# A second written order for the steps of a conv and state-space kernel

## The chip, the cores and the metric

The kernel runs on one core of a Trainium2 chip. The metric is the device time in microseconds of one execution; three runs are given as their median and their range. A profile of one further execution shows every instruction with its start and its length. Five engines work side by side, each with an in-order queue of its own: TensorE (PE in the profile) multiplies matrices, VectorE (DVE) and ScalarE (ACT) work element by element and read TensorE's results, GpSimd (POOL) works element by element on on-chip memory, and SyncE (SP) issues the DMA transfers.

## The reference

The input is x of shape 128 x 128 x 16 x 16 (batch, channels, height, width), in float32. Two layers follow each other.

Layer 0 is a group norm followed by a quantised residual block: batch norm, clipping and rounding to 4 bits, a 3x3 convolution with 4-bit weights masked by a cross pattern, the same again with a diagonal pattern, and two residual additions.

Layer 1 takes each image as 256 tokens of 128 channels:

```python
t = _to_tokens(x)
t = t + mamba(_ln_t(t), fwd weights) + reversed(mamba(reversed(_ln_t(t)), bwd weights))
t = t + moe(_ln_t(t))
x = _from_tokens(t, x)
```

One direction of `mamba` projects the tokens to z, x, B, C and a step size dt; runs a causal convolution of four taps and a silu over x, B and C; takes a softplus of dt; then computes a scan with decay in chunks (as matrix products with an exponential mask), adds D times x, multiplies by silu(z), normalises by the root mean square and projects back to 128 channels with four heads of 64. `moe` is a router over eight experts that keeps the best two of them for each token and mixes their 128 x 128 linear maps with softmax weights.

## The kernel before, in words

Layer 0 runs first, about 300 us, with the whole batch held on chip as 64 tiles of two images; it isn't touched by the change, and neither is any instruction of layer 1.

Layer 1 works on 64 pairs of images (512 tokens each). The work on one pair is written as generators, the `part_...` functions. Each `yield` ends a *step*: a group of instructions that all go to one engine's queue. The parts that matter here:

- `part_a`: load of the pair's tokens, layer norm, transposition to `uT`. `part_c` handles two pairs at once: dt, softplus, logarithms and cumulated sums (`dt` and `r_ps` matmuls), then DMAs that build the rows and columns of the decay mask.
- `part_x` (L821), for direction d and channel block n: one matmul step of 128x512 in float32 into a PSUM bank, one ScalarE step and three VectorE steps (`x1`, `x2`, `x3` below) that are the four taps. The bank is free after the third. `part_z` (L864): a matmul into such a bank, and a silu on ScalarE.
- `part_s` (L905): the mask's exponent as bf16 matmuls into such a bank, then an exponential on ScalarE. `part_g` (L890): the products of B and C, on 64 of the array's 128 rows. `part_m`: VectorE multiplies the two. `part_xt`: four transposes.
- `part_y` (L939): the scan's products, on 64 of the array's 128 columns (128x64), sixteen matmul records; then VectorE adds D times x, GpSimd multiplies by z, ScalarE squares. `part_n`, `part_r`: the root mean square (matmuls on 32 columns, `n` below; then a transpose). `part_o`: the projection back.
- `part_e` (L1024), a long chain: layer norm, transposition (`u2T`), router matmul on 32 columns (`rt`), transpose, then some twenty short VectorE steps on 128x32 values that find the best two experts (`lg`, `mx0`, `sel0`, `seld0`, `fi0`, `sele0`, `lgm`, `mx1`, `sel1`, ..., `g1`, `gt`), one GpSimd power, a transpose (`gtT`), and a DMA of the gates to DRAM. `part_p` loads the gates of two experts spread over all partitions (`gb`) and multiplies them by `u2T` on GpSimd, in two steps. `part_f` (L1116): the residual's transpose (`fT`) and eight expert matmul steps (`f0` to `f7`) into one bank, then out.

PSUM banks come from three rotating sets (L653): two banks for `x`, `z` and `s`, two for `y` and `f`, four for the rest. A matmul step that wants a bank waits until the bank's last reader is done.

The order is written out by hand in the table `T`. For each part it has two lists of places, one for even and one for odd pairs; the place of a step of pair i is `i // 2 * PERIOD` plus the number in the table, with `PERIOD = 372`. A period holds exactly 372 steps, those of two pairs at different stages, so a place is a rank and not a time:

```python
steps += [(i // 2 * PERIOD + t, len(steps) + n, stream) for n, t in enumerate(places[i % 2])]
steps.sort(key=lambda step: step[:2])
```

The steps are then issued in this order (`manual_schedule`), and each engine's queue has its own steps in the order of the places. Waits between engines are put in for data and for buffers.

Of the kernel before, what the change touches and what calls it, by code (L numbers as in the profile page):

```python
# [34 lines left out]
def kernel(ctx: ExitStack, tc: tile.TileContext, a: dict):  # L35
# [311 lines left out]
    with tc.tile_pool(name="w1p", bufs=1) as w1p:  # L347
# [15 lines left out]
        with tc.tile_pool(name="setup1", bufs=1) as setup, tc.tile_pool(  # L363
# [50 lines left out]
            for c in range(4):  # L414
# [34 lines left out]
                n = cuts[c + 1] - cuts[c]  # L449
# [666 lines left out]
    def part_f(i):  # L1116
# [7 lines left out]
        for e in range(NE):  # L1124
# [9 lines left out]

    PERIOD = 372
    T = {
        ('a',): [[72, 128, 230, 236, 267, 307], [250, 319, 407, 437, 469, 473]],
        ('c',): [
            [482, 492, 505, 516, 529, 550, 558, 571, 574, 577, 597, 603, 610, 617, 646, 648, 649, 656, 658,
             668, 688, 695, 706, 723, 727, 752, 774, 785, 887, 997],  # L1140
        ],
        ('x', 0, 0): [[662, 669, 670, 684, 685], [844, 852, 856, 859, 865]],
        ('x', 0, 2): [[693, 694, 700, 703, 712], [874, 881, 889, 890, 891]],
        ('x', 0, 1): [[714, 722, 733, 739, 740], [904, 908, 913, 915, 926]],
        ('x', 1, 2): [[750, 755, 764, 776, 788], [934, 945, 948, 952, 959]],
        ('x', 1, 0): [[771, 775, 790, 792, 797], [960, 968, 973, 978, 981]],
        ('x', 1, 1): [[811, 818, 823, 827, 830], [1001, 1007, 1019, 1023, 1027]],
        ('z', 1, 0): [[836, 839], [1031, 1035]],
        ('bc',): [[858, 892], [1046, 1055]],
        ('sx', 0): [[860], [1059]],  # L1150
        ('z', 0, 0): [[851, 853], [1038, 1043]],
        ('sx', 1): [[868], [1062]],
        ('z', 1, 1): [[863, 867], [1047, 1053]],
        ('z', 0, 1): [[878, 883], [1068, 1077]],
        ('g', 0): [[895], [1110]],
        ('s', 0, 0, 0): [[884, 885], [1079, 1080]],
        ('xt', 0, 0): [[910, 918], [1082, 1114]],
        ('s', 0, 1, 0): [[898, 903], [1083, 1089]],
        ('s', 0, 0, 1): [[909, 914], [1093, 1103]],
        ('s', 0, 0, 2): [[917, 923], [1104, 1121]],  # L1160
        ('m', 0, 0): [[931, 947], [1120, 1130]],
        ('xt', 1, 0): [[905, 935], [1132, 1153]],
        ('s', 0, 1, 1): [[933, 941], [1117, 1126]],
        ('s', 1, 1, 0): [[942, 953], [1133, 1141]],
        ('s', 0, 1, 2): [[967, 970], [1161, 1165]],
        ('xt', 0, 1): [[936, 958], [1088, 1125]],
        ('s', 1, 0, 2): [[1005, 1008], [1173, 1178]],
        ('g', 1): [[996], [1177]],
        ('m', 0, 1): [[1006, 1009], [1189, 1191]],
        ('s', 1, 0, 0): [[979, 988], [1166, 1171]],  # L1170
        ('s', 1, 1, 1): [[998, 999], [1193, 1196]],
        ('xt', 1, 1): [[1000, 1003], [1187, 1192]],
        ('s', 1, 0, 1): [[987, 991], [1182, 1184]],
        ('m', 1, 1): [[1037, 1045], [1209, 1218]],
        ('s', 1, 1, 2): [[1014, 1026], [1201, 1210]],
        ('y', 0, 1): [[1012, 1022, 1025, 1087], [1200, 1204, 1219, 1258]],
        ('y', 0, 0): [[1024, 1029, 1032, 1106], [1207, 1212, 1220, 1269]],
        ('m', 1, 0): [[1017, 1036], [1198, 1221]],
        ('y', 1, 1): [[1052, 1064, 1108, 1113], [1233, 1241, 1254, 1293]],
        ('y', 1, 0): [[1070, 1098, 1109, 1118], [1251, 1278, 1297, 1300]],  # L1180
        ('n', 0): [[1123], [1301]],
        ('n', 1): [[1131], [1312]],
        ('r',): [[1134, 1145, 1149, 1152, 1158], [1322, 1334, 1336, 1338, 1349]],
        ('o', 0): [[1155, 1172], [1337, 1356]],
        ('o', 1): [[1163, 1174], [1348, 1357]],
        ('e',): [
            [1185, 1203, 1205, 1215, 1222, 1227, 1229, 1243, 1245, 1247, 1248, 1266, 1268, 1271, 1272, 1274,
             1284, 1299, 1304, 1310, 1311, 1323, 1326, 1327, 1328, 1329, 1333, 1343, 1344, 1355, 1365],
            [1374, 1387, 1388, 1405, 1411, 1416, 1420, 1441, 1443, 1446, 1448, 1457, 1462, 1464, 1473, 1474,
             1479, 1488, 1491, 1500, 1501, 1507, 1509, 1510, 1512, 1516, 1522, 1526, 1528, 1531, 1540],  # L1190
        ],
        ('p', 0): [[1422, 1433, 1463], [1542, 1578, 1586]],
        ('p', 1): [[1367, 1421, 1426], [1624, 1651, 1655]],
        ('f',): [
            [1445, 1453, 1468, 1469, 1487, 1511, 1548, 1558, 1566, 1569, 1681],
            [1614, 1637, 1660, 1664, 1668, 1688, 1707, 1734, 1754, 1757, 1802],
        ],
        ('p', 2): [[1376, 1472, 1539], [1551, 1606, 1610]],
        ('p', 3): [[1514, 1547, 1552], [1663, 1730, 1736]],
    }  # L1200
    parts = {
        "a": part_a, "c": part_c, "x": part_x, "bc": part_bc, "sx": part_sx, "z": part_z, "xt": part_xt, "g": part_g,
# [45 lines left out]
```

## Time and profile before

| What | us |
|---|---|
| median of three runs | 2683.2 |
| range of the runs | 2682.34 to 2685.82 |
| the profiled execution | 2683.28 |
| its span in the profile | 2681.6 |
| TensorE matmuls busy | 2524.4 |
| VectorE busy | 2386.9 |
| ScalarE busy | 2043.1 |
| GpSimd busy | 1660.4 |

The span runs from the first to the last instruction; the rest of the execution's time lies around it. A busy time is the sum of the times at which an engine has a record; the records of neighbouring instructions can overlap, and the end of a matmul is modelled. In lines of the profile, `out<-in` names tiles, `128*64` behind a matmul is the part of the array that it uses (rows by columns), L is a line of the kernel, and a bracket holds the idle time ahead of an instruction and what ended it.

### The profile page before, as it was taken

Reading aid. Unit: us, or ns where it says so; the run is one execution under the profiler, and the core shown is the slowest. Engines: PE = TensorE matmul, PEld = TensorE weight load, DVE = VectorE, ACT = ScalarE, POOL = GpSimd, SP = SyncE. Lnnn points to the kernel's source line nnn. Section 1 sums busy time; section 2 is a strip of 40 time slices with the busy share of each in tenths; the row PEclk is TensorE's granted clock in tenths of the full one; section 3 lists DMA queues with packets and bytes.
Section 4 is the critical chain, followed back from the end, with each engine's and each line's share of the span. In section 5 each row is a group of like instructions: output and inputs, shape, how many; then the busy total and the mean of one; then the engine's idle time right before and its main releaser. Section 6 shows DMA issues by size and latency. Waiting matters only on the chain.

```text
span 2681.6 us, 47685 instructions
## 1 busy us (share of the span) xinstructions
PE 2524.4 (94%) x16004; PEld 1488.5 (56%) x16004; DVE 2386.9 (89%) x6161; ACT 2043.1 (76%) x3682; POOL 1660.4 (62%) x1728
## 2 busy tenths in 40 slices
PE   0889589999999999999999999999999999999997
PEld 0335245556566665666666556666665666666663
DVE  8877589999999999999999999999999999999884
ACT  6877478887777778777777887777778877777771
POOL 1876315666666666666666666666666666666666
PEclk9989799999999999999999999999999999999998
DMA  8458311332333222333332232323223233232223
GB/s 273 154 201 286 120 35 60 90 94 85 96 90 95 78 86 97 89 93 96 93 94 79 88 95 86 95 92 93 81 84 96 91 90 97 92 96 81 77 88 105
DMA packets 165706, 275.58 MB, mean 103 GB/s; under 512 B 46529, under 2 KB 89537, under 8 KB 165441
## 3 DMA queue, kind: packets, MB, share of 16 engines
q1 hardware_dynamic: 165440, 272.32, 32.6%
q8 instruction: 132, 2.16, 0.3%
q14 instruction: 134, 1.09, 0.1%
HBM read 197.45 MB, written 58.03 MB: 95 GB/s over the span
## 4 chain that ended last, share of the span: by engine, by line
PE 65%; DVE 26%; DMA 3%; issue 2%; ACT 2%; POOL 1%; SPq 0%; DVEq 0%; POOLq 0%; ACTq 0%
PE f_ps L1125 12%; PE x_ps L824 9%; PE o_ps L1008 8%; DVE xc L842 6%; PE y_ps L948 6%; PE z_ps L867 5%; PE cv L221 4%; PE sg L913 3%; DVE yg L960 3%; PE xt_ps L879 3%; PE g_ps L898 3%; PE y_ps L954 3%; DVE bc L842 3%; PE sg L915 2%; DMA xr<-in_x 2%
## 5 line engine op out<-in xcount | busy, mean ns | idle before, releaser
L842 DVE SCALAR_TENSOR_TENSOR xc<-x_ps,cw,xc 128x510 f32<-128x510 f32 (+2 forms) x768 | 570.3, 743 | 99.1 <-ACT xc L836 86.4
L1113 POOL TENSOR_TENSOR gb<-gb,u2T 128x512 f32<-128x512 f32 x512 | 639.8, 1276 | 13.7 <-DMA gb<-gd 12.8
L964 POOL TENSOR_TENSOR yg<-yg,z 128x512 f32<-128x512 f32 x256 | 328.0, 1281 | 502.8 <-DVE yg L960 502.8
L675 ACT ACTIVATE e<-sg 128x512 f32<-128x512 f32 x768 | 449.8, 594 | 223.6 <-PE sg L913 152.7
L1125 PE MATMUL f_ps<-gb,ew 128*128 128x512 f32 x1024 | 524.7, 607 | 3.5 <-POOL gb L1113 3.4
L824 PE MATMUL x_ps<-uT,wx 128*128 128x512 f32 x768 | 403.9, 608 | 9.7 <-DVE bc L842 4.4
L948 PE MATMUL y_ps<-e,xt 128*64 128x256 f32 x2048 | 321.0, 392 | 0.2 <-DVE yg L960 0.2
L929 DVE TENSOR_TENSOR e<-e,g_ps 128x1024 f32<-128x1024 f32 x256 | 310.0, 1211 | 2.8 <-PE g_ps L898 2.8
L842 DVE SCALAR_TENSOR_TENSOR bc<-x_ps,cw,bc 128x510 f32<-128x510 f32 (+2 forms) x384 | 285.1, 742 | 9.0 <-ACT bc L836 3.2
L836 ACT ACTIVATE xc<-x_ps,cb,cw 128x512 f32<-128x512 f32 x256 | 199.1, 778 | 118.1 <-PE x_ps L824 109.6
L867 PE MATMUL z_ps<-uT,wz 128*128 128x512 f32 x512 | 274.9, 619 | 1.3 <-DVE xc L842 1.2
L1008 PE MATMUL o_ps<-wo,yg 128*128 128x128 f32 x2048 | 249.9, 275 | 0.0
L1008 PEld LDWEIGHTS o_ps<-wo,yg 128*128 128x128 f32 x2048 | 239.3, 192 | 19.0 <-DVE sel L1093 17.3
L1125 PEld LDWEIGHTS f_ps<-gb,ew 128*128 128x128 f32 x1024 | 174.3, 192 | 90.5 <-issue 71.4
L973 POOL TENSOR_TENSOR sq<-sq,sq 128x512 f32<-128x512 f32 x128 | 163.3, 1276 | 72.3 <-ACT sq L967 72.2
L954 PE MATMUL y_ps<-e,xt 128*64 128x128 f32 x2048 | 198.9, 273 | 0.0
L960 DVE SCALAR_TENSOR_TENSOR yg<-xc,dcol,y_ps 128x512 f32<-128x512 f32 x256 | 189.1, 739 | 9.7 <-PE y_ps L954 9.7
L221 PE MATMUL cv<-hpad,wq 128*128 128x512 bf16 x640 | 179.4, 423 | 19.2 <-DVE hpad L194 9.7
L913 PE MATMUL sg<-rows,cols 128*128 128x256 bf16 x1024 | 191.5, 274 | 4.7 <-ACT e L675 3.1
L675 ACT ACTIVATE z<-z_ps 128x512 f32<-128x512 f32 x256 | 153.3, 599 | 52.1 <-PE z_ps L867 41.4
L954 PEld LDWEIGHTS y_ps<-e,xt 128*64 128x64 f32 x2048 | 147.0, 137 | 74.1 <-DVE e L934 0.4
L879 PEld LDWEIGHTS xt_ps<-ident,xc 128*128 128x128 f32 x1024 | 128.2, 141 | 105.4 <-issue 99.6
(255 smaller groups left out, 4869.0 us busy)
## 6 DMA issues: line engine op xcount, KB each, us to landing
gb<-gd SPq DMA_DIRECT2D x256, 512.0 KB
xr<-in_x SPq DMA_DIRECT2D x64, 256.0 KB
y<-yt SPq DMA_DIRECT2D x64, 256.0 KB
yt<-y SPq DMA_DIRECT2D x64, 256.0 KB
cc<-bc SPq DMA_DIRECT2D x128, 128.0 KB
out<-ob SPq DMA_DIRECT2D x64, 256.0 KB
o<-o SPq DMA_DIRECT2D x59, 256.0 KB
q<-o SPq DMA_DIRECT2D x59, 256.0 KB
```

The lines of the kernel that those rows point to most:

```text
L221: nc.tensor.matmul(ps, wq[:, tap, q, :], low(hp)[:, :, dy : dy + 16, dx : dx + 16], start=(n == 0), stop=(n == len(passes) - 1),)
L675: nc.scalar.activation(out, in_, func)
L824: nc.tensor.matmul(ps, wx[d][:, n * P : (n + 1) * P], uTs[i], start=True, stop=True)
L842: nc.vector.scalar_tensor_tensor(acc[:, :, to], raw[:, :, of], cw[:, d, n, 3 - back : 4 - back], acc[:, :, to], ALU.mult, ALU.add,)
L867: nc.tensor.matmul(ps, wz[:, d, n * P : (n + 1) * P], uTs[i], start=True, stop=True)
L929: nc.vector.tensor_tensor(e0.rearrange("p h t l -> p h (t l)"), e0.rearrange("p h t l -> p h (t l)"), gps[i, d, k][:, 0:NT].unsqueeze(1).t ...
L948: nc.tensor.matmul(y_ps[64 * q : 64 * q + 64, k, :], xt[:, 2 * k + s0, 64 * h : 64 * h + 64], e0[:, h].rearrange("p t l -> p (t l)"), star ...
L954: nc.tensor.matmul(y_ps[64 * q : 64 * q + 64, k, s1 * P : (s1 + 1) * P], xt[:, 2 * k + s1, 64 * h : 64 * h + 64], e1[:, h, :], start=False ...
L964: nc.gpsimd.tensor_tensor(yg, yg, zs[i, d][:, n, :], ALU.mult)
L1008: nc.tensor.matmul(o_ps[:, (2 * j + d) * P : (2 * j + d + 1) * P], ygs[i, d, n][:, t * P : (t + 1) * P], wo[d][:, n, :], start=(n == 0), s ...
L1113: nc.gpsimd.tensor_tensor(gb[:, e], gb[:, e], u2Ts[i], ALU.mult)
L1125: nc.tensor.matmul(f_ps, ew[:, e, :], gbs[i, e], start=False, stop=(e == NE - 1))
```

## The change

Every list in `T` is replaced: the same parts and the same number of steps in each, at other places. `PERIOD`, the parts and all other code stay. The rows that are spoken of later:

```diff
-        ('x', 0, 2): [[693, 694, 700, 703, 712], [874, 881, 889, 890, 891]],
-        ('x', 0, 1): [[714, 722, 733, 739, 740], [904, 908, 913, 915, 926]],
-        ('x', 1, 2): [[750, 755, 764, 776, 788], [934, 945, 948, 952, 959]],
...
+        ('x', 0, 2): [[799, 803, 811, 815, 817], [973, 983, 994, 996, 999]],
+        ('x', 0, 1): [[829, 835, 848, 849, 857], [1012, 1026, 1033, 1042, 1044]],
+        ('x', 1, 2): [[871, 876, 882, 888, 892], [1048, 1057, 1063, 1064, 1070]],
...
-        ('y', 0, 1): [[1012, 1022, 1025, 1087], [1200, 1204, 1219, 1258]],
-        ('y', 0, 0): [[1024, 1029, 1032, 1106], [1207, 1212, 1220, 1269]],
...
+        ('y', 0, 1): [[1126, 1149, 1156, 1167], [1311, 1320, 1327, 1407]],
+        ('y', 0, 0): [[1130, 1146, 1147, 1172], [1310, 1319, 1326, 1342]],
...
+        ('p', 0): [[1484, 1505, 1508], [1667, 1678, 1690]],
+        ('p', 1): [[1500, 1569, 1591], [1703, 1735, 1757]],
         ('f',): [
...
+            [1554, 1568, 1580, 1607, 1610, 1624, 1651, 1661, 1671, 1677, 1679],
+            [1721, 1752, 1764, 1768, 1783, 1810, 1835, 1855, 1866, 1868, 1895],
         ],
...
+        ('p', 2): [[1556, 1619, 1648], [1730, 1762, 1817]],
+        ('p', 3): [[1649, 1652, 1670], [1772, 1842, 1850]],
```

Sorted by place, TensorE's steps of one period in the repeating middle of the layer are these 103, first before and then after. Steps on a part of the array are in capitals with a star (`Y*` 128x64, `G*` 64x128, `N*`, `RT*`, `DT*` 128x32); `dtT`, `nT`, `rtT`, `gtT` are single transposes:

```
before:
s x xt s N* f4 x nT o gtT s o s s f5 G* s x f6 xt s f7 Y* s Y* z uT u2T x z DT* RT* Y* z fT rtT x dtT z
Y* s f0 G* s x xt s xt f1 s f2 f3 s x xt s f4 N* x f5 nT o s gtT o s s f6 G* s xt x s f7 uT Y* s Y* z
u2T x z r RT* z Y* x z rtT Y* fT s f0 xt s x xt s f1 f2 s G* f3
after:
s f7 Y* Y* z u2T x z RT* Y* z rtT r x z fT Y* G* s xt f0 s x xt s f1 uT s f2 f3 s x xt s N* f4 x nT gtT
o s o s s f5 G* s f6 s xt x f7 s Y* Y* z uT x u2T z DT* Y* RT* z x dtT fT rtT z Y* s G* s f0 x s xt f1
f2 s xt f3 s x xt s N* f4 x nT o s o gtT s f5 s G* s xt s f6 x
```

VectorE's steps of the same period; `x1(dn)` is the first tap of the part ('x', d, n), `m0` and `m1` are `part_m`, `t2` is `part_o`, `yg` is `part_y`, `abn` and `bbn` are the statistics of the two layer norms, the rest is `part_c` and `part_e`:

```
before:
seld1 fi1 m0 sele1 e2 m1 x1(12) g1 g1r e2m gt x2 selm rr gta x3 x1(10) x2 x3 t2 t2 bbn m0 m1 x1(11) m0
x2 x3 yg m0 yg m1 m1 x1(00) x2 x3 yg abn lg mx0 sel0 dtr x1(02) x2 x3 seld0 fi0 sele0 lgm ex mx1 yg sel1
x1(01) x2 x3 seld1 w1 m0 fi1 sele1 e2 w1s m1 x1(12) eq x2 g1 g1r e2m gt x3 selm rr w1a gta x1(10) lwa x2
x3 rec t2 t2 lwm bbn m0 m1 m0 lwm2 x1(11) dt lwmax yg x2 x3 yg daz m1 m0 x1(00) m1 x2 x3 p0 abn yg l0 lg
x1(02) mx0 x2 sel0 p1 x3 seld0 fi0 sele0 l1 yg p2 lgm mx1 x1(01) sel1 x2 x3
after:
m1 daz m0 x1(11) m1 x2 x3 m0 m1 yg yg abn x1(00) x2 x3 yg lg p0 mx0 sel0 l0 seld0 x1(02) fi0 x2 p1 x3
sele0 lgm mx1 sel1 seld1 fi1 sele1 e2 yg l1 x1(01) x2 g1 x3 m0 g1r e2m m1 gt selm gta x1(12) p2 x2 rr x3
x1(10) x2 x3 t2 t2 bbn m0 m1 m0 x1(11) x2 m0 x3 yg yg m1 m1 x1(00) x2 x3 yg abn dtr lg ex mx0 x1(02)
sel0 x2 x3 seld0 fi0 yg w1 sele0 lgm mx1 w1s sel1 eq seld1 x1(01) w1a x2 x3 fi1 m0 sele1 e2 lwa rec m1
lwm x1(12) x2 g1 lwm2 g1r x3 e2m rr gt dt selm gta x1(10) x2 x3 t2 t2 lwmax bbn m0
```

The other three queues are reordered in the same way: ScalarE's, GpSimd's, and the 21 steps of a period in which SP issues DMAs.

## The prediction

> **What bounds the kernel now.** I read the page first: the busy shares, the slices and the chain.
>
> ```profile
> span 2681.6 us, 47685 instructions
> PE 2524.4 (94%) x16004; PEld 1488.5 (56%) x16004; DVE 2386.9 (89%) x6161; ACT 2043.1 (76%) x3682; POOL 1660.4 (62%) x1728
> PE   0889589999999999999999999999999999999997
> PE 65%; DVE 26%; DMA 3%; issue 2%; ACT 2%; POOL 1%; SPq 0%; DVEq 0%; POOLq 0%; ACTq 0%
> ```
>
> From slice 6 on TensorE never falls under nine tenths: that is the planned loop. In the table of stages, 1500 to 2000 us has TensorE busy 498.46 of 500, VectorE 466.47, ScalarE 397.00, GpSimd 321.94, at a granted clock of 1.00. So TensorE sets the loop, with VectorE close behind. The first `o` step of a period starts at 1539.31 and, three periods on, at 1754.64: 71.78 us a period of two pairs, 32 periods.
>
> A busy TensorE may still lose time inside its records, so I read its timeline by starts (columns: start, length, engine, line). Records overlap; what an instruction costs is the distance to the next start.
>
> ```profile
> 1499.80 1.02 PE L1125 MATMUL f_ps<-gb,ew 128*128 128x512 f32 x2
> 1500.76 0.64 PE L981 MATMUL n_ps<-sq,chosen 128*32 128x128 f32 x16
> 1501.33 1.12 PE L824 MATMUL x_ps<-uT,wx 128*128 128x512 f32 x2
> 1502.29 1.02 PE L1125 MATMUL f_ps<-gb,ew 128*128 128x512 f32 x2
> 1503.15 0.27 PE L989 MATMUL n_ps<-ident,ns 128*128 128x128 f32 x1
> ...
> 1512.54 0.65 PE L948 MATMUL y_ps<-e,xt 128*64 128x256 f32 x4
> 1513.02 0.39 PE L954 MATMUL y_ps<-e,xt 128*64 128x128 f32 x4
> 1513.24 0.60 PE L948 MATMUL y_ps<-e,xt 128*64 128x256 f32 x4
> 1513.67 0.39 PE L954 MATMUL y_ps<-e,xt 128*64 128x128 f32 x4
> 1513.99 0.39 PE L913 MATMUL sg<-rows,cols 128*128 128x256 bf16 x2
> 1514.31 0.65 PE L948 MATMUL y_ps<-e,xt 128*64 128x256 f32 x4
> ```
>
> The same `f` pair takes 0.86 (1502.29 to 1503.15) before a whole-array step, 0.96 before the 128*32 step. `x` behind that step takes 0.96; elsewhere 0.86. In `y`, 0.48 on arrival against 0.43, and 0.32 on leaving against 0.22. An `s` between two `y` takes 0.32, not 0.22. So a change of array shape costs 0.10 on the instruction before it, and behind it 0.10 (`x`, `z`, `f`), 0.05 (`y`, `n`, `rt`, `dt`, four-transposes) or 0.01 (`s`).
>
> There is one regular wait too; TensorE, VectorE and GpSimd timelines:
>
> ```profile
> 1534.81 0.39 PE L915 MATMUL sg<-rows,cols 128*128 128x512 bf16 x1 [0.22 <-DVE xc L842]
> ...
> 1530.10 1.26 DVE L1075 SCALAR_TENSOR_TENSOR lg<-sel,lg 128x32 f32<-128x32 f32 x1
> 1532.15 1.16 DVE L1065 TENSOR_TENSOR sel<-lg,mx 128x32 f32<-128x32 f32 x1
> 1533.23 1.51 DVE L842 SCALAR_TENSOR_TENSOR xc<-x_ps,cw,xc 128x508 f32<-128x508 f32 x2
> ...
> 1529.98 1.32 POOL L964 TENSOR_TENSOR yg<-yg,z 128x512 f32<-128x512 f32 x1 [3.47 <-DVE yg L960]
> 1531.99 1.28 POOL L973 TENSOR_TENSOR sq<-sq,sq 128x512 f32<-128x512 f32 x1 [0.68 <-ACT sq L967]
> ```
>
> The `s` needs a bank that a convolution is still draining. The `f` ahead of it began at 1533.46 and would have cost 0.96; `s` starts at 1534.81, 0.39 late, once a period. VectorE was late because two tiny router steps (0.18 elsewhere) took 1.26 and 1.16: each ends as a 1.3 us GpSimd step ends.
>
> **What the Trainium skill says.** "TensorEngine Tiling (Array Packing)", Key Properties: changing the tiling mode drains TensorE, another tile of the same mode does not. The trace agrees: 0.10 on leaving, nothing from one half of `y` to the next (0.22). "TensorE: Matmul & The Clock Gate", Step-by-step: weight loads are pulled ahead, matmuls stay in order; so a late `s` holds all behind it, as the 0.39 does. "SBUF — State Buffer", Who interferes with whom: a VectorE instruction with two SBUF inputs and a GpSimd one that reads SBUF exclude each other. The rows above agree.
>
> **The change part by part.** No instruction is added or removed. A period has 372 steps before and after, the counted activation-table switches stay at four, and TensorE's steps are the same 103. Only the orders of the five queues move.
>
> (1) *Shape changes.* From the two orders printed above, read round the loop: 31 changes before, 26 after. Before: 31 departures x 0.10 = 3.10; arrivals at `x`, `z`, `f` 8 x 0.10 = 0.80, `fT` 0.05, `s` 6 x 0.01 = 0.06, partial steps 16 x 0.05 = 0.80: 4.81 us. After: 2.60; 6 x 0.10 = 0.60; 5 x 0.01 = 0.05; 15 x 0.05 = 0.75: 4.00. Saved 0.81 a period, 0.162 for each change. Check: steps at their bare spacings (`x` 12 x 0.86, `z` 8 x 0.86, `f` 16 x 0.86, `o` 4 x 1.79, `y` 8 x 1.30, `g` 4 x 0.70, `xt` 8 x 0.44, `s` 24 x 0.22, six four-transposes x 0.44, the rest 3.88) give 66.6; with 4.81 and the wait of 0.39, 71.8: the measured period. Over the whole layer the table gives 996 changes before, 835 after: 161 x 0.162 = **26 us**. Nothing hides it, since TensorE is the bound.
>
> Not seen before: `y` straight behind `y` (twice a period). Between 0, as for its halves, and 0.15 each: 0 to 10 us; I take 0. New pairs of partial shapes (`y` to `g`, `dt` to `y`, `y` to `rt`): `rt` to `y` is in the trace (0.33 and 0.48) and costs about the common price, so I take that, give or take 0.1 each: 10 us either way.
>
> (2) *The wait of 0.39.* On VectorE `lgm` and `mx1` stand just ahead of the convolution ('x',0,1) of even pairs and `sel1` inside it. In the new VectorE order `e2`, `yg`, `l1` stand ahead and only `g1` (0.16, one SBUF input) inside; in odd pairs `sel1`, `eq`, `seld1` ahead and `w1a` (0.2, two inputs) inside. I take the wait as gone: 32 x 0.39 = **12 us**, with 0 as the other end.
>
> (3) *New waits.* TensorE arrives 1.2 us earlier per period, 70.6; VectorE's 67.0 of records are then 95%. The tightest new place I find is where the router's and the step sizes' work of one half meets: ('x',0,2) of an odd pair, then dtT, fT, rtT, z, y, s, g, and the `s` of the even pair that wants the bank: 0.86+0.11+0.44+0.11+0.96+1.45+0.33+0.85 = 5.1 us. Draining takes 1.06 to the start of ScalarE's step (1510.07 to 1511.13), 0.78 there, 3 x 0.74 on VectorE: 4.1. Margin 1.0, and `sel0` is inside it: 0.18, or 1.16 if blocked. Behind that `s` stand all of TensorE's queue, and ScalarE's exp. I take 0.2 a period, 0 to 0.4: **6 us** back.
>
> (4) *SP, ScalarE and GpSimd.* The same loads in another order; the shortest stretch in table places from a `gb` load to its first product falls from 11 to 3 (p 3, even). SP runs ahead of the others, so what counts is when a buffer frees: here f1 at place 1580, 72 places (14 us) before the product, against 3.65 us for this load at the end of the trace's chain. That hides it; were it exposed, GpSimd's product and f6 would be late by up to 3.65. cc, the row and column loads, `yt` and `out` keep several us as well. I cost this, and the queues of ScalarE (80% busy) and GpSimd (64%), at nothing. Filling and draining keep nearly the same order: 0, give or take 4.
>
> Sum, on the profiled execution's 2683.28 (span 2681.6, 1.7 around it; the median of the runs is 2683.2): 2683.3 - 26 - 12 + 6 = **2651 us**.
>
> **Rivals.** *A, VectorE takes over.* The 5% that it has left is uneven; banks free late and half the gain turns into waits of `s`, `x` and `z`. For: 93% busy, only two banks. Against: its records overlap (1.21 long, 1.13 apart for L929), so it has more room than its share says. A period of about 71.3: 2683 - 32 x 0.48 = 2668.
> *B, the gain is all eaten.* New waits of 1.2 us a period: 2683. It is also where we end if the price of a change is really the refill of a pipe that must wait anyway; against it speaks that the waits view shows TensorE waiting 3.1 us in 1000.
> *C, slower.* The shared port. In the new VectorE order of odd pairs `sel0` sits in ('x',0,2), `lgm` and `sel1` ahead of ('x',0,1) and `w1a` in it. If GpSimd's 1.28 us products now fall on them, each costs about 1.1 while a convolution holds or wants a bank. Four a period are 4.4; the margins at these two places (1.0 above, and 0.9 from ('x',0,1) to ('x',1,2): x, s, xt, f, f, s, xt, f, s are 5.0 against 4.1) take nearly half; 2.2 exposed less the 1.2 saved is +1.0 x 32: 2715. It decides from 1.2 us exposed a period. For: before already pays about 3.9 (one `lgm` 1.07, `sel` 0.98 and 0.72, L779 1.1) and exposes 0.39. Against: that is the same total chance, and most such steps found GpSimd idle.
> That the changes do not fall is excluded by the count.
>
> **How the numbers follow.** Likeliest (0.62): 2651, its own range 2638 to 2664 from the ends in (1) to (3). A 0.17; B 0.07; C 0.14. Faster by over 0.2% (about what a measurement of this kernel can tell from no change) 0.79, within it 0.07, slower 0.14. The range 2638 to 2690 holds all but most of C and a little below: about 0.83.
>
> **What would show it.** Right: a period near 70.6 between `o` starts; `y` behind `y` at 0.43 and 0.22; the 0.39 gone; TensorE still at 99%. A: waits of `s` on L842 several times a period. C: L1065, L1075 or L1068 at 1.2 more than five times a period. Wrong in (1): `y` to `g` or `y` to `rt` losing over 0.25. Wrong in (4): TensorE's f_ps or GpSimd's products waiting for DMA.

## The result, and the profile after

The changed kernel takes 2648.4 us (median of 4 runs, 2644.5 to 2651.4) against 2683.4 of the kernel before on the same chip: ratio 0.9867, 95% interval 0.985 to 0.9885. The forecast was 2651. The profiled execution took 2651.35 and its span is 2649.6, 32.0 less than before's 2681.6. From the page of the kernel after: span, busy times and the shares of the chain.

```profile
span 2649.6 us, 47721 instructions
PE 2499.6 (94%) x16004; PEld 1493.9 (56%) x16004; DVE 2416.2 (91%) x6161; ACT 2030.1 (77%) x3682; POOL 1654.9 (62%) x1728
PE 84%; DVE 7%; POOL 3%; ACT 2%; issue 2%; DMA 1%; SPq 0%; POOLq 0%; DVEq 0%; ACTq 0%
```

As many matmul records as before take 24.8 us less. VectorE has the same 6161 records and is busy 29.3 us longer (the part on the rivals says where), yet it holds less of the chain (7% where it had 26%); its regular wait is gone.

Measured between the starts of `r`, which comes once a period, before's 27 periods have a mean of 71.757 us and after's 27 a mean of 70.570. That is 27 x 1.187 = 32.0 us. Filling up to the first of these `r` takes 1.75 longer, what follows the last takes 1.7 less. So the gain lies in the loop. (Where nothing differs ahead of it, in the kernel before and in experiment 4, the first `r` starts at 327.4 and 322.1, so 2 us in the filling say nothing.) TensorE's timeline in the kernel after (start, length):

```profile
1497.46 0.39 PE L954 MATMUL y_ps<-e,xt 128*64 128x128 f32 x4
1497.68 0.60 PE L948 MATMUL y_ps<-e,xt 128*64 128x256 f32 x4
1498.12 0.39 PE L954 MATMUL y_ps<-e,xt 128*64 128x128 f32 x4
...
1505.07 0.27 PE L1044 MATMUL rt_ps<-ident,rts 128*128 128x128 f32 x1
1505.17 1.03 PE L784 MATMUL r_ps<-sums,daz 128*128 128x256 f32 x4
1506.04 0.38 PE L787 MATMUL r_ps<-ident,lwz 128*128 128x128 f32 x2
...
1509.87 0.39 PE L954 MATMUL y_ps<-e,xt 128*64 128x128 f32 x4
1510.18 0.92 PE L898 MATMUL g_ps<-cc,bc 64*128 64x256 f32 x8
1511.04 0.39 PE L913 MATMUL sg<-rows,cols 128*128 128x256 bf16 x2
```

Read by starts: where one `y` follows another (1497.46 to 1497.68 to 1498.12) the steps cost 0.22 and 0.44, the same as inside a `y`. Where `g` follows `y`, `y` leaves at 0.31 and `g` takes 0.86: the common price. The first part of `r` (L784) takes 0.87 here; it took 0.97 before, with whole-array matmuls ahead of it and behind it in both kernels.

A period without any wait takes 70.40 in the kernel after. Some are longer, up to 70.9, irregularly. From its waits view between 400 and 2600 us (total us, times, longest):

```profile
PE sg L913 <- DVE sel L1068: 4.0, 13, 0.4
```

That is the `s` behind `g` of even pairs, the tightest place that the prediction named. (`sel` L1068 stands just behind the convolution on VectorE.)

### The profile page after: what moved, and what is told of

It reads as the page before. It is cut to its first block, busy times and chain, and to the rows that moved or that the text cites. A ratio compares the mean times of both kernels' runs of the same rounds, so it can differ in the third digit from the quotient of the medians.

```text
span 2649.6 us, 47721 instructions
## 1 busy us (share of the span) xinstructions
PE 2499.6 (94%) x16004; PEld 1493.9 (56%) x16004; DVE 2416.2 (91%) x6161; ACT 2030.1 (77%) x3682; POOL 1654.9 (62%) x1728
## 3 DMA queue, kind: packets, MB, share of 16 engines
q1 hardware_dynamic: 165440, 272.32, 32.7%
## 4 chain that ended last, share of the span: by engine, by line
PE 84%; DVE 7%; POOL 3%; ACT 2%; issue 2%; DMA 1%; SPq 0%; POOLq 0%; DVEq 0%; ACTq 0%
PE f_ps L1125 16%; PE x_ps L824 12%; PE o_ps L1008 9%; PE y_ps L948 8%; PE z_ps L867 8%; PE sg L913 4%; PE xt_ps L879 4%; PE y_ps L954 4%; PE g_ps L898 4%; PE cv L221 4%; PE sg L915 2%; POOL xr L591 1%; PE n_ps L981 1%; DVE bc L842 1%; PE u_ps L710 1%
## 5 line engine op out<-in xcount | busy, mean ns | idle before, releaser
L1113 POOL TENSOR_TENSOR gb<-gb,u2T 128x512 f32<-128x512 f32 x512 | 646.5, 1279 | 130.5 <-DMA gb<-gd 112.6
L913 PE MATMUL sg<-rows,cols 128*128 128x256 bf16 x1024 | 197.1, 274 | 9.0 <-DVE sel L1068 4.0
L824 PEld LDWEIGHTS x_ps<-uT,wx 128*128 128x128 f32 x768 | 131.9, 193 | 118.1 <-issue 59.4
L996 POOL TENSOR_TENSOR rr<-rr,mhalf 128x8 f32<-128x8 f32 x64 | 105.4, 1647 | 142.8 <-DVE rr L992 142.8
```

The lines of the kernel that those rows point to most:

```text
L824: nc.tensor.matmul(ps, wx[d][:, n * P : (n + 1) * P], uTs[i], start=True, stop=True)
L913: nc.tensor.matmul(sg[:, :, of], c_[:, k, d, s, half, :], r_[:, :, d, t, of], start=True, stop=True)
L1113: nc.gpsimd.tensor_tensor(gb[:, e], gb[:, e], u2Ts[i], ALU.mult)
```

## Experiments

All edits are lines set behind the table `T`; only places change, no instruction does. The numbers 6 and 7 stand for no run. Gains are given per period where the trace allows it, since all periods of one kernel are nearly alike.

### 1. Kernel before, `s` taken out from between the two `y`

```diff
+    T['s', 1, 1, 2][0][0] = 1011.5    # was 1014
+    T['s', 1, 1, 2][1][0] = 1199.5    # was 1201
```

> The order before, with one TensorE step moved: the s step between two y steps goes ahead of both, twice a period. 868 shape changes in place of 996; nothing else in any queue moves. If a change of array shape costs what I priced (0.10 for a departure, 0.05 for an arrival at y, 0.01 at s), each place saves 0.26 us, so 2683 - 2 x 32 x 0.26 = 2667, with the once-a-period wait of s on a convolution still there. If the gain of the change came from its waits and buffers alone, this run stays at 2683.

Measured: 2690.8 us, ratio 1.0035 (1.0021 to 1.0049). Slower. TensorE has 27 changes a period and saves 0.51 around the two places, as priced (0.52). But the period is 72.00, 0.22 longer. `r` is now late: it starts 1.44 behind the start of the `z` ahead of it, where that was 0.97. TensorE, VectorE and GpSimd timelines of this kernel, and then a line of its waits view (total us, times, longest):

```profile
1523.62 1.13 PE L784 MATMUL r_ps<-sums,daz 128*128 128x256 f32 x4 [0.43 <-DVE e L934]
...
1518.73 0.75 DVE L960 SCALAR_TENSOR_TENSOR yg<-xc,dcol,y_ps 128x512 f32<-128x512 f32 x1 [0.39 <-PE y_ps L954]
...
1521.70 1.27 DVE L779 TENSOR_SCALAR lwz<-lw 128x64 f32<-128x64 f32 x1
1522.89 0.67 DVE L934 TENSOR_TENSOR e<-e,g_ps 128x512 f32<-128x512 f32 x1
...
1521.65 1.27 POOL L964 TENSOR_TENSOR yg<-yg,z 128x512 f32<-128x512 f32 x1 [0.82 <-DVE yg L960]
```

```profile
PE r_ps L784 <- DVE e L934: 11.9, 28, 0.4
```

`r` wants a bank that the product L934 (`m1` of ('m', 1, 0)) still reads; that product ends at 1523.56 and `r` starts at 1523.62. Two possible causes stand ahead of it in VectorE's queue: `yg`, which waits 0.39 for the later `y`, and `lwz` (L779), 1.27 us long. I took the first at the time. A second loss, 0.26, is an `s` that waits for ScalarE's exponential; 0.47 and 0.26 lost, 0.51 saved, give the 0.22.

### 2. Kernel after, `z` put back between the two `y`

```diff
+    T['z', 1, 0][0][0] = 938.5     # was 943
+    T['z', 1, 1][1][0] = 1128      # was 1132
```

> The order after, with the z step that followed two y steps moved between them, twice a period: 961 shape changes in place of 835, no other queue moved. By the price of a change: two departures (0.20), an arrival at y (0.05) and at the transposes behind (0.05) more at each place, 0.30 x 2 x 32 = 19 us slower than the order after: 2648 + 19 = 2667. If shape changes are free, 2648. A slower result with new waits of z or x in the trace would count for neither.

Measured: 2663.2 us (ratio to before 0.9934, 0.9913 to 0.9954), 14.8 above the kernel after. 30 changes a period instead of 26; the waitless period is 70.98, so four changes cost 0.58 where 0.60 was priced, with no new wait in it: this is the price of the shapes alone. The medians differ by less than the 19 expected mostly because the scattered waits of the `s` behind `g` became fewer here (4 and 1.4 us, for 13 and 4.0).

### 3. Kernel after, `sel0` out of the convolution

```diff
+    T['e',][0][10] = 1371.5    # was 1367
```

> The order after, with one short VectorE step (sel0) moved from inside the convolution ('x',0,2) of odd pairs to behind its third tap. If the scattered waits of s behind g come from sel0 being held up by GpSimd's 1.28 us products while the bank is taken, they vanish (their extra comes to 5.7 us in the trace after), the time falls to about 2643 and the runs lie closer together than the 2644 to 2651 of the order after. If the waits come from a late convolution for another reason, the time stays at 2648 and the waits stay.

Measured: 2646.6 us (0.9863, 0.9847 to 0.988), the same as the kernel after within its interval. Six waits of the `s` behind `g` remain, 2.0 us in all where there were 13 and 4.0. `sel0` is at most part of it. What else stands there is seen in the kernel after itself, in VectorE's, GpSimd's and TensorE's timelines, first a period with the wait and then one without it:

```profile
1896.57 1.30 DVE L746 SCALAR_TENSOR_TENSOR ex<-dtr 128x64 f32<-128x64 f32 x1
1898.54 0.18 DVE L1065 TENSOR_TENSOR sel<-lg,mx 128x32 f32<-128x32 f32 x1
1896.51 1.28 POOL L1113 TENSOR_TENSOR gb<-gb,u2T 128x512 f32<-128x512 f32 x1 [0.86 <-PE rt_ps L1044]
1900.33 0.38 PE L913 MATMUL sg<-rows,cols 128*128 128x256 bf16 x2 [0.41 <-DVE sel L1068]
...
2108.73 0.92 DVE L746 SCALAR_TENSOR_TENSOR ex<-dtr 128x64 f32<-128x64 f32 x1
2108.29 1.27 POOL L1113 TENSOR_TENSOR gb<-gb,u2T 128x512 f32<-128x512 f32 x1 [0.48 <-DMA gb<-gd]
```

`ex`, just ahead of the convolution that has to free the bank, ends as the GpSimd product ends, after 1.30 or 0.92; `sel0` (L1065) takes 0.18 in the bad period. Over all periods of this trace between 400 and 2600 us it is nearly always `ex`: in 12 of the 13 with the wait `ex` takes 1.07 to 1.30 and `sel0` 0.18, in one `ex` takes 0.21 and `sel0` 1.10, and in those without the wait neither takes more than 0.92. The six waits of experiment 3 all stand behind an `ex` of 1.13 or more. Whether the `s` waits depends on when the product starts, by less than half a microsecond. GpSimd is idle ahead of it in both periods, so that is set by what the product waits for, a load of `gb` in the second. In the first the view names a transpose of TensorE; the product reads only `gb` and `u2T`, so a load is likelier there too. Experiment 12 takes `ex` out.

### 4. Kernel before, `sel1` out of the convolution

```diff
+    T['e',][1][16] = 1484.5    # was 1479
```

> The order before, with one short VectorE step (sel1) moved from inside the convolution ('x',0,1) of even pairs to behind its third tap; TensorE's order and its 996 shape changes stay. If sel1 (1.16 us when GpSimd holds it up) is what makes s late by 0.39 once a period, the wait goes and 32 x 0.39 = 12 us with it: 2671. If lgm ahead of the convolution (1.26) is the cause, the wait stays: 2683. If shape changes are the whole of the gain of the change, waits of this size are covered elsewhere: 2683 as well, but with the wait gone from the trace.

Measured: 2667.7 us (0.9947, 0.993 to 0.9964). The period is 71.39 instead of 71.78: exactly the 0.39 of the wait, and nothing came in its place. (The median fell by more than 32 x 0.39; what differs outside the loop, such as the start of the first `r`, varies by some us.) The table of stages of this kernel between 1000 and 2000 us has TensorE busy without a gap:

```profile
sum 1000.00, PE 1000.00 PEld 606.81 DVE 939.75 ACT 798.70 POOL 647.32; mean PE 1000.00 PEld 606.81 DVE 939.75 ACT 798.70 POOL 647.32
```

So before without its wait (71.39) and after without waits (70.40) both leave no gap in TensorE's records, and differ by 0.99. The count of shapes priced 0.81. In the kernel before, `r` and the `z` ahead of it each take about 0.11 more than their like, 0.22 in sum; in the kernel after `r` takes 0.87, and the step ahead of it, now `rtT`, its usual 0.10. One `x` takes 0.90 there for 0.86, 0.04 the other way. That makes up the rest; experiments 5 and 14 ask about `r`.

### 5 and 8. Kernel before, `r` later; and the same with the `s` out

```diff
+    T['c',][0][19] = 675.5     # r, was 668 (both)
+    T['s', 1, 1, 2][0][0] = 1011.5    # 8 only
+    T['s', 1, 1, 2][1][0] = 1199.5    # 8 only
```

> The order before, with the r_ps step of the decay (L784) moved behind the next router and z steps, once a period; its neighbours on both sides use the whole array in both places, and the count of shape changes stays at 996. In the trace before, the z ahead of it costs 0.97 and it costs 0.97 itself, each 0.10 above the bare spacing, without any change of shape; its weights were loaded only at 1518.99, when a bank came free, and not ahead. If a late weight load costs the same 0.2 as a shape change, it goes: 2683 - 32 x 0.2 = 2677. If this step is simply dearer, or the bank is late there too, 2683.

> The order before with both: s ahead of the two y steps (868 shape changes) and r_ps later. With s moved alone, the 0.5 a period that it saved came back as a wait of r_ps for its bank. If that wait is the whole reason, here the saving stays: 0.52 + 0.2 a period, 2683 - 23 = 2660. If an earlier TensorE always finds another engine late, the time stays at 2683 or above with a wait at another place.

Measured: 2688.7 and 2689.9 us (both 1.0025, 1.0015 to 1.0036), periods 72.02 and 71.89. Both misses. (The count of changes stays as said, but a step on part of the array stands behind `r` in both places: the router's, then a `y`.) From the waits view of 5, then of 8:

```profile
PE z_ps L867 <- ACT z L675: 8.6, 30, 0.4
```

```profile
PE rt_ps L1037 <- DVE e L934: 14.4, 28, 0.5
```

In 5, `r` takes 0.86 and the `z` ahead of it only the price of its shapes, but that `z`, the one behind `r` before, now comes 1.4 us earlier and its own bank isn't free: `r` had covered that. In 8 the bank that L934 frees goes to `rt` in `r`'s place, and `rt` waits for the same product. Moving the step that waits only handed the wait on, so what frees the bank has to come earlier.

### 9. Kernel before, `s` out, `r` later, `sel1` out

```diff
+    T['e',][1][16] = 1484.5    # besides the three lines of 8
```

> The order before with three steps moved: s ahead of y, r_ps later, sel1 out of the convolution. If shape changes, the late weight load and the wait of s are separate terms that add up, 0.52 + 0.2 + 0.39 a period: 2683 - 35 = 2648, all of the gain of the change with four table entries of a period's 372. If they overlap, since VectorE becomes the bound (rival A), 2660 to 2670 with new waits of s, x or z.

Measured: 2676.9 us (0.998, 0.9974 to 0.9987), period 71.50: that of 8 less 0.39. The two losses are independent, but `rt` still waits, and the 2648 that their sum promised is far off.

### 10. Kernel after, both held-up steps out and two more changes of shape saved

```diff
+    T['e',][0][10] = 1371.6              # sel0, was 1367
+    T['c',][0][4] = 627.5                # ex, was 615
+    T['c',][0][5] = 627.6                # its exponential, was 626
+    T['c',][0][0] = 596.5                # dt next to rt, was 595
+    T['s', 0, 1, 0][0][0] = 1003.5       # s behind g, was 1000
```

> The order after with four steps moved: dt behind the y that stood between it and the router step (both 32 columns wide, so two changes of shape fewer in sum with its neighbours, one net), s behind g instead of between y and g in one of the two halves, and the short VectorE steps ex and sel0 from ahead of and inside the convolution ('x',0,2) to behind it. 774 shape changes in place of 835: 61 x 0.16 = 10 us; and the scattered waits, 4.6 us in sum, gone: 2648 - 15 = 2634. If the waits have another cause, 2638; if VectorE is the bound by now, 2648.

Measured: 2638.1 us (0.9834, 0.9821 to 0.9847), faster than both kernels, 10.3 below after. Every period of the steady loop is 70.15 or 70.16, with 24 changes. The table of stages, 1000 to 2000 us:

```profile
sum 1000.00, PE 1000.00 PEld 619.21 DVE 959.49 ACT 806.74 POOL 657.56; mean PE 1000.00 PEld 619.21 DVE 959.49 ACT 806.74 POOL 657.56
```

VectorE at 96% still takes nothing from TensorE. The time is the one expected if the waits had another cause, but the waits are gone; what is missing to 2634 is in the two changes of shape, which experiment 12 separates.

### 11. Kernel before, `s` out, `sel1` out, `yg` behind the convolution

This tests my first reading of experiment 1: that `yg`, waiting for `y`, holds up the product.

```diff
+    T['y', 0, 1][0][1] = 1027.5    # yg, was 1022
+    T['y', 0, 1][0][2] = 1027.6    # GpSimd's product, was 1025
+    T['s', 1, 1, 2][0][0] = 1011.5
+    T['s', 1, 1, 2][1][0] = 1199.5
+    T['e',][1][16] = 1484.5
```

> The kernel before, with three groups of steps moved: the s that stands between two y (place 1014) goes ahead of them, as in the first experiment; sel1 goes behind its convolution, as in the fourth; and on VectorE yg(0,1) goes from in front of the second convolution half of ('x',1,1) to behind its third part, so that VectorE does not stand waiting for y while that convolution could run. Theory (the two changes of shape were saved in the first experiment too, and what ate them was VectorE's queue: yg(0,1), waiting 0.39 for y, holds the convolution, daz, lwz and the product that frees r's bank): that wait goes, r starts at most 0.1 late, and the period is 71.8 - 0.39 - 0.4 = about 71.0, so 2683 - 32 x 0.79 = 2658 us, with 2652 to 2664 as its ends. Rival (VectorE is simply full there, and what stands ahead of the product is late for its own work, not for a wait): r stays 0.4 late, the period is 72.0 - 0.39 = 71.6, and the time about 2677 us.

Measured: 2699.4 us (2686 to 2713; 1.0061, 1.0035 to 1.0088), outside both expectations. `yg` no longer waits, and yet `r` is later than ever (28 waits, up to 1.8, 24.1 us in sum). VectorE's and GpSimd's timelines of this kernel:

```profile
1594.43 2.06 DVE L776 TENSOR_TENSOR daz<-dt,aneg 128x32 f32<-128x32 f32 x2
1596.41 1.30 DVE L779 TENSOR_SCALAR lwz<-lw 128x64 f32<-128x64 f32 x1
1593.94 2.50 POOL L964 TENSOR_TENSOR yg<-yg,z 128x512 f32<-128x512 f32 x2 [4.49 <-DVE yg L960]
1596.39 3.74 POOL L1113 TENSOR_TENSOR gb<-gb,u2T 128x512 f32<-128x512 f32 x3
```

Each `yg` releases a GpSimd product of 1.27 us. With the two `yg` in a row, their two products run in a row, and a product of `gb` follows. `daz` (two instructions) and `lwz` stand next in VectorE's queue: 2.06 and 1.30 here, where they take 0.29 and 0.19 when GpSimd is idle. In most periods the first `daz` (0.83) and `lwz` (1.26) are caught (period 71.75); in some, as here, both `daz` fall under the two `yg` products and `lwz` under that of `gb` (72.92): hence the wide spread of the runs. Since this edit took a wait away and put conflicts in its place, it does not decide between the two readings; it points to the second, `lwz` under a GpSimd product. Experiment 13 decides.

### 12. Kernel after, only `ex` and `sel0` out

```diff
+    T['e',][0][10] = 1371.6    # sel0
+    T['c',][0][4] = 627.5      # ex
+    T['c',][0][5] = 627.6      # its exponential
```

> The kernel after, with ex, the step after it in its chain, and sel0 of odd pairs moved on VectorE behind the convolution ('x',0,2) that they stand ahead of or in; TensorE's order is not touched. Theory (the scattered waits of s behind g come from ex, and sel0, held up by a GpSimd product just ahead of that convolution): the waits of s on sel go, every period takes 70.4, and the run is 2648.4 less about 4.5 = 2644 us, with its runs closer together than the 7 us of the kernel after; so of the 10 us that the tenth kernel gained over after, 4 to 5 were waits and the rest the two changes of shape. Rival (the waits come from VectorE being full, wherever these steps stand): periods stay scattered up to 70.9, and the time stays at 2646 to 2649 us.

Measured: 2644.8 us (2643.0 to 2646.8; 0.9857, 0.9844 to 0.9869). All periods in the steady loop are 70.38 to 70.41 and the `s` behind `g` waits no more. By shapes kept apart, VectorE's group of `ex` in 1000 to 2000 us of this kernel (busy, mean ns):

```profile
L746 DVE SCALAR_TENSOR_TENSOR ex<-dtr 128x64 f32<-128x64 f32 x14 | 3.0, 215 | 0.0
```

215 ns against 898 in the kernel after. So of the 10.3 us between the medians of experiment 10 and after, 3.7 go to these waits and 6.7 to the two changes of shape. The intervals of 12 and after overlap; the periods tell them apart, 70.40 in every one for a mean of 70.57. The two changes bring 70.15 for 70.40, 0.25, where two at the average of 0.16 come to 0.32. Priced by kind it is 0.26: 0.10 and 0.05 for the one at `dt`, 0.10 and 0.01 for the one at `s`.

### 13 and 14. Kernel before, `daz` and `lwz` ahead of `yg`; 13 with `s` and `sel1` out too

```diff
+    T['c',][0][18] = 656.5     # daz with lwz, was 658 (both)
+    T['s', 1, 1, 2][0][0] = 1011.5    # 13 only
+    T['s', 1, 1, 2][1][0] = 1199.5    # 13 only
+    T['e',][1][16] = 1484.5           # 13 only
```

> The kernel before, with the s taken out from between the two y as in the first experiment, sel1 behind its convolution as in the fourth, and one step more moved on VectorE: daz with lwz goes ahead of yg(0,0) instead of behind it. Theory: what makes the product that frees r's bank late is lwz, which takes 1.27 us instead of 0.19 because yg(0,0) has just released a GpSimd product that runs over it; ahead of yg(0,0) GpSimd is idle, lwz takes 0.2 or little more, the product ends about 0.8 earlier and r no longer waits (0.43 in the first experiment). The period is then 72.0 - 0.39 - 0.5 = about 71.1, 71.0 to 71.3, and the time 2683 - 32 x 0.7 = 2661 us, with 2657 to 2668 as its ends. Rival (VectorE has no room there in any order, or the GpSimd product falls on another step of the same stretch): r or the step behind it stays late by 0.4, period 71.6, 2677 us or more.

> The kernel before, with daz and lwz alone moved on VectorE ahead of yg(0,0). TensorE's order and its 996 changes of shape stay. Theory: the 0.2 us a period that the change gained beyond the count of shapes came from the late weight load of r (0.10 on the z ahead, 0.10 on r itself), whose bank is freed late because lwz stands under a GpSimd product; with lwz out of it the weights are loaded ahead, z and r take 0.86 or 0.87 each, the period is 71.78 - 0.2 = 71.58, and the time 2677 us. Rival (the 0.2 has another cause, or the GpSimd product falls on something as pressing): period 71.78 or more, 2683 us or more.

Measured: 2658.6 us (0.9912, 0.9899 to 0.9926) and 2675.2 us (0.9973, 0.9963 to 0.9984), as the theory had them. In 13 `yg` still waits for the later `y`, and `lwz`, now ahead of the second `yg`, is short; VectorE's timeline of 13:

```profile
1500.77 0.75 DVE L960 SCALAR_TENSOR_TENSOR yg<-xc,dcol,y_ps 128x512 f32<-128x512 f32 x1 [0.40 <-PE y_ps L954]
1503.07 0.19 DVE L779 TENSOR_SCALAR lwz<-lw 128x64 f32<-128x64 f32 x1
```

`r` starts there 0.86 behind its `z`, without a wait. So the wait of `yg` alone does not make `r` late; with `lwz` out from under the GpSimd product `r` is on time.

Run 14 moves one VectorE step by one place. TensorE's timeline and its weight loads in the kernel before:

```profile
1518.02 1.02 PE L867 MATMUL z_ps<-uT,wz 128*128 128x512 f32 x2
1518.99 1.13 PE L784 MATMUL r_ps<-sums,daz 128*128 128x256 f32 x4
...
1518.99 0.73 PEld L784 LDWEIGHTS r_ps<-sums,daz 128*128 128x128 f32 x4 [0.77 <-DVE e L934]
```

The same in run 14:

```profile
1512.28 1.02 PE L867 MATMUL z_ps<-uT,wz 128*128 128x512 f32 x2
1513.13 1.03 PE L784 MATMUL r_ps<-sums,daz 128*128 128x256 f32 x4
...
1512.71 0.19 PEld L784 LDWEIGHTS r_ps<-sums,daz 128*128 128x128 f32 x1 [0.24 <-issue]
```

Before, the first weights of `r` load only when its bank is free, at the moment its matmul starts; in 14 they load 0.42 ahead, under `z`. `z` then costs 0.85 and not 0.97, `r` 0.87 and not 0.97, and the period falls from 71.78 to 71.56. No wait of TensorE's matmuls shows this loss: it sits inside two records.

Run 13 has a period of 70.92: 71.78, less 0.39 (`sel1`), less 0.22 (`lwz`), less 0.25 for the two `s`. Those are 0.51 of shapes and 0.26 given back once a period; TensorE's and ScalarE's timelines of run 13:

```profile
1533.46 1.02 PE L1125 MATMUL f_ps<-gb,ew 128*128 128x512 f32 x2
1534.58 0.38 PE L913 MATMUL sg<-rows,cols 128*128 128x256 bf16 x2
1533.92 0.60 ACT L675 ACTIVATE e<-sg 128x512 f32<-128x512 f32 x1
```

`f` should cost 0.86 and costs 1.12, since the `s` moved forward wants a bank that the exponential of an earlier `s` reads until 1534.52.

## Why the prediction was right, point by point

**(1) Shapes.** The price holds where nothing else moves: 0.58 for 0.60 in experiment 2, 0.51 gross for 0.52 in 13, 0.25 for 0.26 in 10 against 12. It is a price by kind, 0.11 to 0.20 a change; the 0.162 is only the mean of the five that this change saves. The unknowns came out as taken: `y` behind `y` free, `y` to `g` at the common price. Where the step missed is the loop's floor: 0.99 a period was gained and 0.81 was counted. I had read the 0.97 of `z` ahead of `r`, and of `r`, over and did not ask why whole-array steps among whole-array steps cost 0.10 more. It is a weight load that waits for a bank. In the kernel before, `lwz` under a GpSimd product makes that bank late (experiment 14). The kernel after has `lwz` free as well, but there it is the place of `r` that does it. The last VectorE product L934 ahead of `r` in the kernel after:

```profile
1500.00 0.68 DVE L934 TENSOR_TENSOR e<-e,g_ps 128x512 f32<-128x512 f32 x1
```

It ends 4.4 us before the first weights of `r` load, at 1505.07, and they wait for no engine; in the kernel before it ended as they began.

Why short steps are held up at all: "SBUF — State Buffer", Who interferes with whom, in the Trainium skill says that a `tensor_scalar` can enter a mode that takes the port shared with GpSimd, and that an instruction with two SBUF inputs contends with a GpSimd one that reads SBUF: `lwz` is of the first kind, as are L688 of the layer norm (`abn`) and L1085 (`g1`); `ex` and the `sel` steps are of the second. VectorE's groups by shape in 1000 to 2000 us agree; first those of the kernel before, then those of the kernel after (busy us, mean ns of one):

```profile
L1065 DVE TENSOR_TENSOR sel<-lg,mx 128x32 f32<-128x32 f32 x56 | 33.9, 606 | 0.5
L779 DVE TENSOR_SCALAR lwz<-lw 128x64 f32<-128x64 f32 x14 | 17.8, 1274 | 0.0
L1068 DVE TENSOR_TENSOR sel<-sel,desc 128x32 f32<-128x32 f32 x56 | 10.1, 180 | 0.0
L688 DVE TENSOR_SCALAR rstda<-mva 128x4 f32<-128x4 f32 x28 | 6.7, 238 | 1.0
L1085 DVE TENSOR_SCALAR g<-e 128x4 f32<-128x4 f32 x27 | 4.3, 158 | 0.0
L746 DVE SCALAR_TENSOR_TENSOR ex<-dtr 128x64 f32<-128x64 f32 x14 | 3.0, 217 | 0.0
```

```profile
L1065 DVE TENSOR_TENSOR sel<-lg,mx 128x32 f32<-128x32 f32 x56 | 20.2, 360 | 1.0
L1068 DVE TENSOR_TENSOR sel<-sel,desc 128x32 f32<-128x32 f32 x56 | 19.8, 353 | 0.5
L688 DVE TENSOR_SCALAR rstda<-mva 128x4 f32<-128x4 f32 x29 | 16.9, 583 | 1.0
L1085 DVE TENSOR_SCALAR g<-e 128x4 f32<-128x4 f32 x28 | 14.6, 521 | 0.0
L746 DVE SCALAR_TENSOR_TENSOR ex<-dtr 128x64 f32<-128x64 f32 x14 | 12.6, 898 | 0.0
L779 DVE TENSOR_SCALAR lwz<-lw 128x64 f32<-128x64 f32 x15 | 2.8, 188 | 0.0
```

The new order moved the GpSimd products from some small steps to others: `lwz` and some of the L1065 came free; `ex`, `seld` (L1068), L688 and L1085 were caught.

**(2) The wait of 0.39.** Right, and measured alone in experiment 4: 0.39 a period, by moving `sel1`.

**(3) New waits.** 0.2 a period was allowed; after's mean of 70.57 over its floor of 70.40 is 0.17. The place was the one named. The mechanism was named too, a short step held up by a GpSimd product, but with the wrong step: of the 13 waits `sel0` made one and `ex`, which stands ahead of the same convolution in the order printed and was left out, twelve. With `sel0` moved, `ex` still made six; with both moved, there is none. `ex` alone was not moved.

**(4) The other queues.** Costing them at nothing held for TensorE. On GpSimd the argument that the loads stay hidden was wrong, and the sign set for it came. Waits of GpSimd for `gb`, in the whole run, before and then after:

```profile
POOL gb L1113 <- DMA gb<-gd: 12.8, 12, 6.9
```

```profile
POOL gb L1113 <- DMA gb<-gd: 112.6, 74, 6.6
```

The loads have become nine times as exposed on GpSimd, which is 62% busy and has the room (why they land later was not looked into); TensorE waited for such a product once in 2200 us, for 0.4. But these loads help to place the product over `ex`: what cost came back came by the port, not by TensorE waiting for the data.

The sum, by the loop's 27 intervals instead of 32 periods: shapes 27 x 0.81 = 21.9, `r`'s weights, less the 0.04 of the `x`, 27 x 0.18 = 4.9, the wait 27 x 0.39 = 10.5, new waits 27 x 0.17 = 4.6 back: 32.7 against the 32.0 measured. The forecast of 32 had 26 and 12 less 6. So the counts over the whole layer were a little too large for what filling and draining let through, which together gave nothing, and the gain of `r`'s weights, not foreseen, filled that gap. That part of the closeness is luck. What filling lost and draining gained (1.75 and 1.7) was not looked into.

**The rivals.** A: VectorE went to 481 us of 500 between 1500 and 2000 and TensorE still has 498.26 there; what little is lost in the loop is one port conflict, and experiments 10 and 12 have no such wait there. B fell with the 0.17 of (3) and with experiment 2. C was right that the conflicts would grow, and wrong in how much of them would show. With two more groups of the same views (L1075: 20.3 before, 18.9 after; L1089: 4.4 and 10.0) the six above took 100.5 us in 1000 before and 115.8 after, about 1.0 more a period: that is VectorE's longer busy time. Short steps of over 0.6 us came to 4.0 a period before and 5.9 after. But C needs 1.2 exposed a period, and 0.17 is: in the loop TensorE has hardly a wait behind the others. Where the conflicts hold up a bank they cost more: experiment 11 has the edits of 13 but for the places of `daz`, `lwz` and one `yg`, and its periods are 0.8 to 2.0 us longer.

## What to carry to other kernels

Price a change of array shape from the starts of the records on both sides, and check the sum against the period: here 0.11 to 0.20 us each, by the kinds of the two steps, held in both directions. Moving TensorE's steps alone in the kernel before made it slower (experiments 1, 5, 8), because in each case a step came to wait for a bank, twice the one that a single VectorE product frees; look at what stands ahead of that product in its queue, above all at a short step that takes 1.3 us (it was so in 1 and 8). A whole-array matmul that costs 0.1 more than its like is a question to ask: it may be a weight load waiting for a bank.

## What the runs showed of the hardware that I had not expected

- A late weight load cost about 0.1 on the step ahead and 0.1 on its own step, as much as a change of shape, without any wait of a matmul in the record (0.97 and 0.97 before, 0.85 and 0.87 in run 14). "TensorE: Matmul & The Clock Gate", Step-by-step, has weight loads pulled ahead; the trace shows what it costs where they can't be.
- One VectorE step of 128x64, 0.19 long, decides 0.22 us of TensorE's period by its place ahead of or behind the instruction that starts GpSimd (run 14). Where products follow each other in a row, one caught step more costs 1.17 (run 11: periods of 72.92 and 71.75).
